# A hand-written issue order for TensorE, VectorE and ScalarE in the first layer of a graph network

## The chip, the cores and the metric

One core of a Trainium2 chip. The time is the device time of one execution in microseconds; the kernel before took 6855.91 us, the median of three runs (6827.99 to 6860.81). In the profile PE is TensorE (PEld its weight loads), DVE VectorE, ACT ScalarE, POOL GpSimd (here: it issues gathers), SP SyncE (here: it issues the other transfers).

## The reference, cut to what matters

Two layers of a graph network over 3125 nodes of 256 features and 100000 edges. The change is in layer 0, whose first half adds two independent parts to `x`:

```python
def transformer_conv(x, edge_index, ...):          # twice, each followed by batch norm and leaky ReLU
    q, k, v = (x @ wq + bq), (x @ wk + bk), (x @ wv + bv)       # 4 heads of 64
    alpha = jnp.sum(q[dst] * k[src], axis=-1) / math.sqrt(out_ch)
    # softmax of alpha over the edges of each dst node
    out = jax.ops.segment_sum(v[src] * alpha[..., None], dst, num_segments=n)
    return out + x @ ws + bs

for i in range(4):                                  # the linear attention, "mix"
    h = _layernorm(x, ln1_g[i], ln1_b[i])
    # q: softmax over features, k: softmax over tokens; context = k^T v, out = q context
    x = x + _linear_attn(h, Wq[i], Wk[i], Wv[i], Wo[i], bo[i])
    h = _layernorm(x, ln2_g[i], ln2_b[i])
    x = x + (gelu(h @ W1[i] + b1[i]) @ W2[i] + b2[i])
```

After that come a routed mixture of experts and layer 1, which the change leaves alone.

## The kernel before, in words

Everything is float32. The kernel is written against a framework with a scheduler: the program states instructions and their tiles, and the scheduler decides the order in each engine's queue. At run time each engine goes through its queue in order and waits on semaphores.

**The convolution.** Nodes are sorted by degree and packed 128 to a tile, 25 tiles (`SLOTS` has the number of edge slots of each, 64 down to 22, 833 in all). `by_slots` goes over the tiles; `steps` cuts a tile's slots into 2 to 4 steps of one or two halves of up to `SUB` = 8 slots, 63 steps and 115 halves for each convolution. For each slot `gather` (L635) issues one indirect transfer on POOL that brings the 128 rows `k|v` of the edges' sources into a buffer `kv` of 8 slots. There are four `kv` buffers. On a half, DVE multiplies the keys by the query (L926) and sums over features into `al` (L930). On a step, DVE adds the bias, takes the maximum and subtracts it (L939, L943, L944), ACT takes the exponential (L952), DVE sums it into `den` (L953). On a half again, DVE multiplies the values by the weights (L959) and adds pairs of slots (L965), and PE adds the slots up with an identity matmul into `acc` (L968), which frees the `kv` buffer. ACT copies `acc` into `res` (L972). At the tile's end the steps are joined (L978 to L999), and `done` adds the skip product on PE (L1101, L1107), ACT adds the bias, and SP stores `hsp`. Between the convolutions the batch norm, and for each tile a product with the next `k|v` weights that POOL scatters into `kvtab2`; after the second, a transpose and a scatter into `gout`.

**The linear attention** runs beside it. `l0_mix_groups` is a generator over 4 layers and 7 groups of up to 4 row tiles of 125, in two passes for each layer: norm and transposes (`norm_T`, L1176 to L1195), keys with exponential (L1234, L1241), queries and values (L140), the context (L1269), the softmax of the queries, stored to DRAM as `qd` through ACT's queue; then join, attention output (`add`, L1202), norm, the 1024-wide gelu (L1339, L1343) and the second product (L140, L1202). `by_slots` calls `beside` once a step, which lets the generator state a rated number of its units. This sets only where the units stand in the program: the scheduler then merges both into each engine's queue by its own priorities and estimates.

Both parts share PE, DVE and ACT. PSUM has four banks for the attention (`mm`), two for the convolution's sums (`cps`) and two for queries (`qa`).

Of the kernel before, what the change touches and what calls it, by code (L numbers as in the profile page):

```python
# [10 lines left out]
F32 = mybir.dt.float32  # L11
# [8 lines left out]
P = 125  # L20
# [805 lines left out]

class Beside:
# [46 lines left out]
def by_slots(k, order, kvtab, heads, scale, pl, wq, bq, inputs, done, edge=None, fill=None, beside=None):  # L874

# [9 lines left out]
    wide = 2 * SUB * heads  # L885
# [3 lines left out]
    if edge is not None:  # L889
        qq = pq.tile([128, 2, D], F32, name="qa", tag="qa")  # L890

    def prepare(i):
        qa = pq.tile([128, 512], F32, name="qa", tag="qa") if edge is None else None
        q = qq[:, i % 2] if qa is None else qa[:, :D]
        xpT = inputs(i, None if qa is None else qa[:, D:])
        for ci in range(2):
            nc.tensor.matmul(q, xpT[:, ci], wq[:, ci], start=(ci == 0), stop=False)
        nc.tensor.matmul(q, k.ones_row, bq, start=False, stop=True)
        return qa, q, xpT

    for i, ns in enumerate(SLOTS):
        st = steps(ns)
        nC = len(st)
        for t in range(3 * (i == 0) or 1) if fill is not None else ():
            if i + 2 * (i > 0) + t < len(SLOTS):
                fill(i + 2 * (i > 0) + t)
        qa, q, xpT = prepare(0) if i == 0 else ahead
# [4 lines left out]
        for c, subs in enumerate(st):  # L912
# [4 lines left out]
            if edge is not None:  # L917
                add_edges = edge(i, s0, S)
            for m in subs:
# [4 lines left out]
                if edge is not None:  # L924
                    add_edges(kv, b0, m)
# [21 lines left out]
            if edge is None:  # L947
                lo = D + c * wide % D
                w3 = qa[:, lo : lo + S * heads].rearrange("p (s h) -> p s h", h=heads)
            else:  # L950
                w3 = a2
# [22 lines left out]
            if beside is not None:  # L974
                beside()
# [15 lines left out]
        if edge is None:  # L991
            share = qa[:, : nC * heads].rearrange("p (c h) -> p c h", h=heads)
        else:
            share = mx[:, :nC]
# [11 lines left out]
def l0_weights(k, pool, a, n):  # L1006


    nc = k.nc
    wkv = pool.tile([128, 2, 2 * D], F32, name="wkv", tag="wkv")  # L1010
    bkv = pool.tile([128, 2 * D], F32, name="bkv", tag="bkv")
    for j, nm in enumerate("kv"):
        nc.sync.dma_start(
            wkv[:, :, j * D : j * D + D], a[f"w{n}{nm}"].rearrange("(c p) m -> p c m", p=128)
        )
        nc.sync.dma_start(bkv[:, j * D : j * D + D], a[f"b{n}{nm}"].partition_broadcast(128))
    one = lambda f, nm, tag: f(k, pool, a[nm], tag)
    return (
        wkv, bkv, load_w(k, pool, a[f"w{n}q"], f"wq{n}"), load_row(k, pool, a[f"b{n}q"], f"bq{n}"),
        load_w(k, pool, a[f"w{n}s"], f"ws{n}"), load_col(k, pool, a[f"b{n}s"], f"bs{n}"),  # L1020
        load_col(k, pool, a[f"g{n}"], f"gam{n}"), load_col(k, pool, a[f"be{n}"], f"bet{n}"),
    )
# [12 lines left out]
def l0_gnn_slots(k, dram, order, a, y, pp, pq, cw, beside, tmp):  # L1035
# [11 lines left out]
    ws = {1: l0_weights(k, cw, a, 1)}  # L1047
    with ExitStack() as st:
# [11 lines left out]
        wkv, bkv = ws[1][:2]  # L1060
# [12 lines left out]
    ws[2] = l0_weights(k, cw, a, 2)  # L1073
    kvtab2 = dram.tile([NQ * 128, 2 * D], F32, name="kvtab2")
    bst = cw.tile([128, 2, NQ, 6], F32, name="bst")
# [3 lines left out]
    for n in (1, 2):  # L1079
        wq, bq, wsk, bs, gam, bet = ws[n][2:]  # L1080
        hsp = dram.tile([128, NQ, 2, 128], F32, name=f"hsp{n}")
        with ExitStack() as st:
            gp, wp = pl(st, ("c_kv", 4), ("c_wk", 2))

            def inputs(i, ps):
                if n == 1:
                    return rows_T(k, wp, ps, ytab, order.near[:, i : i + 1])
                h = wp.tile([128, 2, 128], F32, name="xg", tag="xg")
                nc.sync.dma_start(h, prev[:, i])
                t = wp.tile([128, 2, 128], F32, name="xpT", tag="xpT")  # L1090
                norm_cols(k, t, h, sc, sh)
                return t

            def done(i, res, nC, xpT):
                ps = pp.tile([128, 512], F32, name="cps", tag="cps")
                o = wp.tile([128, 2, 128], F32, name="o1", tag="o1")
                mm = None
                for c in range(2):
                    ch = slice(c * 128, c * 128 + 128)
                    for s in range(nC):  # L1100
                        m1 = nc.tensor.matmul(  # L1101
                            ps[:, ch], res[:, s, ch], k.ident, start=(s == 0), stop=False
                        )
                        if s == 0 and mm is not None:
                            after(k, m1, [mm])
                    for ci in range(2):
                        mm = nc.tensor.matmul(  # L1107
                            ps[:, ch], wsk[:, ci, ch], xpT[:, ci], start=False, stop=(ci == 1)
                        )
                for c in range(2):  # L1110
                    nc.scalar.activation(
                        o[:, c], ps[:, c * 128 : c * 128 + 128], AF.Identity,
                        bias=bs[:, c : c + 1], scale=1.0,
                    )
                    nc.vector.bn_stats(bst[:, c, i], o[:, c, : min(128, N - i * 128)])
                nc.sync.dma_start(hsp[:, i], o)

            by_slots(
                k, order, (kvtab1, kvtab2)[n - 1], 4, 0.125, (gp, wp, pp, "cps", pq), wq, bq,
                inputs, done, fill=order.fill if n == 1 else None, beside=beside,  # L1120
            )
        prev = hsp
        for c in range(2):
            nc.vector.bn_aggr(bmv[:, c], bst[:, c])
        nc.scalar.activation(sc, bmv[:, :, 1], AF.Sqrt, bias=k.eps, scale=1.0)
        nc.vector.reciprocal(sc, sc)
        nc.vector.tensor_tensor(sc, sc, gam, op=ALU.mult)
        nc.vector.tensor_tensor(sh, bmv[:, :, 0], sc, op=ALU.mult)
        nc.vector.tensor_tensor(sh, bet, sh, op=ALU.subtract)
        with ExitStack() as st:  # L1130
            big, wp = pl(st, ("c_h", 1), ("c_rows", 4))
            h = big.tile([128, NQ, 2, 128], F32, name="h")
            for g0 in range(0, NQ, 5):
                nc.sync.dma_start(h[:, g0 : g0 + 5], hsp[:, g0 : g0 + 5])
            if n == 2:
                gout = dram.tile([NQ * 128, D], F32, name="gout")
            wkv, bkv = ws[2][:2]
            sent = []
            for i in range(NQ):
                norm_cols(k, h[:, i], h[:, i], sc, sh)  # L1140
                ps = pp.tile([128, 512], F32, name="cps", tag="cps")
                if n == 1:
                    t = wp.tile([128, 2 * D], F32, name="kvrow", tag="kvrow")
                    for c in range(2):
                        nc.tensor.matmul(ps, h[:, i, c], wkv[:, c], start=(c == 0), stop=(c == 1))
                    nc.vector.tensor_tensor(t, ps, bkv, op=ALU.add)
                    put_rows(k, kvtab2, order, i, t, sent)
                else:
                    t = wp.tile([128, D], F32, name="row", tag="row")
                    for c in range(2):  # L1150
                        nc.tensor.transpose(ps[:, c * 128 : c * 128 + 128], h[:, i, c], k.ident)
                    nc.scalar.copy(t, ps[:, :D])
                    put_rows(k, gout, order, i, t, sent)
# [6 lines left out]
def l0_mix_groups(k, dram, a, y, wts, one, wp, hp, pp):  # L1160
# [3 lines left out]
    nc, N, NT = k.nc, k.N, k.NT  # L1164
    scale = 32.0 ** -0.25
    NG = len(k.groups)
    ps_tile = lambda: pp.tile([128, 512], F32, name="mm", tag="mm")

    def norm_T(g0, ng, g, b):

        st = wp.tile([P, 4, 6], F32, name="ln_st", tag="ln_st")
        mv = wp.tile([P, 4, 2], F32, name="ln_mv", tag="ln_mv")
        rs = wp.tile([P, 4], F32, name="ln_rs", tag="ln_rs")
        nm = wp.tile([P, 4], F32, name="ln_nm", tag="ln_nm")
        for j in range(ng):
            nc.vector.bn_stats(st[:, j], y[:, g0 + j])  # L1176
            nc.vector.bn_aggr(mv[:, j], st[:, j])
        nc.scalar.activation(rs[:, :ng], mv[:, :ng, 1], AF.Sqrt, bias=k.eps[:P], scale=1.0)
# [22 lines left out]
    def add(i, ps):  # L1201
        nc.vector.tensor_tensor(y[:, i], ps, y[:, i], op=ALU.add)  # L1202

    for l in range(4):
# [118 lines left out]
        for gi, (g0, ng) in enumerate(k.groups):  # L1323
# [12 lines left out]
            for j in range(8):  # L1336
# [9 lines left out]
                if j % 2:  # L1346
                    yield
# [1366 lines left out]
```

## Time and profile before

| what | value |
|---|---|
| median of three runs | 6855.91 us |
| the profiled execution | 6843.34 us, its span 6841.6 us |
| granted TensorE clock, mean | 0.812 of full speed |
| busy over the span | PE 4761 us (70%), DVE 4259 (62%), POOL 2895 (42%), ACT 1565 (23%) |
| first gather of the first convolution | 303 us |
| between the convolutions | 1815 to 1880 us |
| last scatter of layer 0's convolutions | 3462 us |

The page shows the span in slices and the costliest groups of instructions; busy time of PE is counted from pipelined matmuls and is not PE at its peak. Every float32 product of the program shows as two records. The idle time of an engine before an instruction is put down to what released that instruction.

### The profile page before, as it was taken

How to read it: one execution, taken by the hardware profiler on the slowest of the kernel's cores; microseconds unless marked ns; L12 is line 12 of the kernel's file. 1: busy time of each engine (PE TensorE's matmuls, PEld its weight loads, DVE VectorE, ACT ScalarE, POOL GpSimd, SP SyncE). 2: the span in 40 equal slices, each digit the busy share in tenths (PEclk: the TensorE clock that was granted, in tenths of full speed). 3: DMA queues.
4: the chain of work that ended last, by engine and by line, in shares of the span. 5: the costliest groups of instructions: out<-in, count | busy, mean ns of one | idle time of the engine just before them, and what ended most of it. 6: DMA issues, size and time to landing. Idle time of an engine off the chain costs nothing. (4 is left out here: it accounts for less than half of the span.)

```text
span 6841.6 us, 48524 instructions
## 1 busy us (share of the span) xinstructions
PE 4761.2 (70%) x15819; PEld 2715.8 (40%) x15819; DVE 4259.0 (62%) x6249; ACT 1565.2 (23%) x3160; POOL 2894.6 (42%) x2947
## 2 busy tenths in 40 slices
PE   3444887578855797668837757777887877787639
PEld 2233654345533464445525523333333333333215
DVE  5277767666666777767632256666776566667571
ACT  2111223223312233223321102222222222121111
POOL 2456655555455555555442134334443333333210
PEclk9767988789978898779858878788888878777769
DMA  4356555545455555555444354333443333343310
GB/s 137 93 151 188 174 146 167 165 145 156 148 162 158 161 170 158 166 152 161 143 147 130 113 163 127 93 108 116 131 129 119 112 115 104 113 129 111 99 34 20
DMA packets 374153, 908.38 MB, mean 133 GB/s; under 512 B 94264, under 2 KB 169946, under 8 KB 373764
## 3 DMA queue, kind: packets, MB, share of 16 engines
q0 software_dynamic: 232624, 725.48, 36.7%
q1 hardware_dynamic: 132740, 155.30, 7.1%
q10 hardware_dynamic: 8526, 24.39, 0.9%
q8 instruction: 128, 2.10, 0.1%
q14 instruction: 135, 1.11, 0.1%
HBM read 813.50 MB, written 91.30 MB: 132 GB/s over the span
## 5 line engine op out<-in xcount | busy, mean ns | idle before, releaser
L635 POOL DMA_INDIRECT kv<-kvtab,slots x2499 | 2438.8, 976 | 2411.5 <-PE acc L968 819.8
L926 DVE TENSOR_TENSOR kv<-kv,qa 128x1792 f32<-128x1792 f32 (+2 forms) x345 | 716.6, 2079 | 359.8 <-DMA kv<-kvtab,slots 298.4
L2042 DVE TENSOR_TENSOR kv<-kv,e 128x1024 f32<-128x1024 f32 (+1 forms) x448 | 505.4, 1140 | 469.2 <-PE e L2037 199.6
L930 DVE TENSOR_REDUCE al<-kv 128x28 f32<-128x1792 f32 (+5 forms) x345 | 713.1, 2075 | 5.4 <-issue 3.8
L2037 PE MATMUL e<-weT,eaT 128*128 128x512 f32 (+1 forms) x896 | 552.4, 714 | 196.7 <-ACT eaT L2036 98.9
L968 PE MATMUL cps<-kv,ident 128*128 128x256 f32 x1792 | 506.7, 437 | 162.5 <-DVE kv L965 73.6
L968 PEld LDWEIGHTS cps<-kv,ident 128*128 128x128 f32 x1792 | 381.9, 221 | 269.5 <-issue 101.9
L959 DVE TENSOR_TENSOR kv<-kv,qa 128x1792 f32<-128x1792 f32 (+2 forms) x230 | 472.1, 2076 | 0.0
L1339 PE MATMUL mm<-hTm,w 128*128 128x500 f32 (+1 forms) x896 | 389.2, 593 | 64.2 <-issue 34.2
L140 PE MATMUL mm<-w,hid 128*125 128x256 f32 x1600 | 377.6, 387 | 11.8 <-issue 10.9
L965 DVE TENSOR_TENSOR kv<-kv 128x768 f32<-128x768 f32 (+1 forms) x345 | 350.8, 1044 | 1.1 <-DVE cw L1320 1.1
L2037 PEld LDWEIGHTS e<-weT,eaT 128*128 128x128 f32 (+1 forms) x896 | 161.6, 218 | 438.4 <-issue 227.1
L140 PEld LDWEIGHTS mm<-w,hid 128*125 128x125 f32 x1600 | 299.4, 190 | 83.2 <-issue 37.7
L968 PE MATMUL acc<-kv,ident 128*128 128x256 f32 x896 | 257.4, 449 | 67.4 <-DVE kv L965 62.4
L1339 PEld LDWEIGHTS mm<-hTm,w 128*128 128x128 f32 x896 | 175.5, 211 | 260.8 <-issue 211.1
L968 PEld LDWEIGHTS acc<-kv,ident 128*128 128x128 f32 x896 | 200.2, 229 | 146.7 <-DVE kv L965 89.4
L2036 ACT COPY eaT<-e 128x128 f32<-128x128 f32 (+1 forms) x448 | 110.1, 266 | 583.0 <-PE e L2034 265.9
L959 DVE TENSOR_TENSOR kv<-kv,al 128x1792 f32<-128x1792 f32 (+2 forms) x115 | 235.1, 2082 | 0.0
L140 PE MATMUL mm<-wqv,hTm 128*125 128x512 f32 x400 | 224.8, 669 | 5.2 <-DVE qs L1259 5.2
L2034 PE MATMUL e<-ident,ea 128*128 128x128 f32 (+1 forms) x448 | 131.8, 326 | 98.7 <-DVE kv L2042 50.9
L2475 PE MATMUL w<-x,sel 32*128 32x500 f32 (+3 forms) x448 | 168.1, 694 | 45.9 <-ACT sq L2480 28.1
L1234 PE MATMUL mm<-hTm,wk 128*128 128x500 f32 (+1 forms) x224 | 121.3, 684 | 104.7 <-ACT hTm L1195 69.5
(394 smaller groups left out, 7486.1 us busy)
## 6 DMA issues: line engine op xcount, KB each, us to landing
kv<-kvtab,slots POOLq DMA_INDIRECT x2499
w<-in_L_ffn_w_dram SPq DMA_DIRECT2D x32, 512.0 KB
qd<-qT ACTq DMA_DIRECT2D x24, 500.0 KB
kvtab<-st SPq DMA_DIRECT2D x12, 1000.0 KB
qT<-qd SPq DMA_DIRECT2D x24, 500.0 KB
xTg<-xcols SPq DMA_DIRECT2D x24, 500.0 KB
w<-in_L_mix_W_dram SPq DMA_DIRECT2D x8, 1024.0 KB
xs<-zero SPq DMA_DIRECT2D x16, 512.0 KB
```

Source lines behind the costliest of these rows:

```text
L140: nc.tensor.matmul(ps, lhs(c), w(c), start=(c == 0), stop=(bias is None and c == n_chunks - 1))
L635: return k.nc.gpsimd.indirect_dma_start(out=out, out_offset=None, in_=table, in_offset=bass.IndirectOffsetOnAxis(ap=index, axis=0),)
L926: nc.vector.tensor_tensor(kv[:, :m, :D], kv[:, :m, :D], q.unsqueeze(1).to_broadcast([128, m, D]), op=ALU.mult,)
L930: nc.vector.tensor_reduce(al[:, b0 : b0 + m], hv(kv[:, :m, :D]), axis=AX.X, op=ALU.add)
L959: nc.vector.tensor_tensor(v, v, w3[:, b0 : b0 + m].unsqueeze(3).to_broadcast([128, m, heads, d]), op=ALU.mult,)
L965: nc.vector.tensor_tensor(v, v, kv[:, half : 2 * half, D:], op=ALU.add)
L968: nc.tensor.matmul(acc[:, :D], k.ident, kv[:, j, D:], start=(b0 + j == 0), stop=(kv is bufs[-1][2] and j == left[-1]),)
L1339: nc.tensor.matmul(ps[:, :w_], w1[:, c, j * 128 : j * 128 + 128], hT[:, c, :w_], start=(c == 0), stop=(c == 1),)
L2034: nc.tensor.transpose(e[r, 0, :128], ea[:, c0 : c0 + n * 64], k.ident)
L2037: nc.tensor.matmul(e[:, :n].rearrange("p b d -> p (b d)"), eaT[r], weT[r, :n].rearrange("p b d -> p (b d)"), start=True, stop=True,)
L2042: nc.vector.tensor_tensor(t, t, e[:, :n].unsqueeze(2).to_broadcast([128, n, 2, D]), op=ALU.add)
L2475: nc.tensor.matmul(ps[:f, b, :w_], sel[rows, t * 128 : t * 128 + f], qT[rows, :w_], start=True, stop=True, tile_position=((h0 + b) * 32, 0),)
```

## The change

The three engines PE, DVE and ACT get, in the layer-0 stretch, the order in which the program states instructions (`k.tc.manual_schedule(engines=ORDERED)`); POOL and SP stay with the scheduler. For that the program is restated.

- `SlotOrder` replaces `by_slots` for layer 0 and states the steps as a software pipeline: the gathers of step n+1 ahead of step n, the first half's keys of step n+1 at the end of step n, a tile's join and output in the first step of the next tile. Layer 1 keeps `by_slots`.
- `l0_mix_pieces` cuts the attention into pieces: a PE part (`pe`), a closing part on DVE or ACT (`post`), a weight in us of PE time and the pieces that must be closed before.
- `Filling` puts pieces at three places in each step (twice 63 steps) and at one in each of the 25 tiles between the convolutions, by a rate that uses them up at the end. It looks at most 8 pieces ahead for one that may start, and states a piece's closing part behind the next piece's PE part.
- Smaller edits: the context's diagonal blocks alone are kept (32 columns instead of 128), two row tiles of attention output are added at once, `qd` is stored by SP instead of ACT, keys and values have four buffers instead of two, `hTm` two instead of one, and the second convolution's query and skip weights load into the first's buffers.

```diff
+class Filling:
+    def __init__(self, pieces, points, window=8):
+        self.todo, self.window, self.last = list(pieces), window, None
+        self.rate, self.due = sum(p.w for p in self.todo) / points, 0.0
...
+    def one(self):
+        for at, p in enumerate(self.todo[: self.window]):
+            if all(d.done for d in p.deps):
+                break
+        else:
+            return None
+        self.todo.pop(at)
+        if p.pe is not None:
+            p.pe()
+        self.flush()
+        self.last = p
+        return p
+
+    def __call__(self, share=1.0):
+        self.due = min(self.due + share * self.rate, 3.0 * self.rate)
+        while self.due > 0.0:
+            p = self.one()
+            if p is None:
+                self.flush()
+                break
+            self.due -= p.w
...
+class SlotOrder:
...
+        for n, t in enumerate(self.steps):
...
+            if n + 1 < len(self.steps):
+                self.gathers(n + 1)
+            if two:
+                self.keys(n, 1)
+            self.softmax(n)
+            if t["last"]:
+                self.join_max(i)
+            mix()
+            if c == 1:
+                self.q[i + 1] = make()
+            self.values(n, 0)
+            if before:
+                self.join(i - 1)
+            mix()
+            if before:
+                before["out"][0]()
+            if two:
+                self.values(n, 1)
+            if t["last"]:
+                self.join_sum(i)
+            if n + 1 < len(self.steps):
+                self.keys(n + 1, 0)
+            self.result(n)
+            if c == 0:
+                turn()
+            mix()
+            if before:
+                before["out"][1]()
+            if c == 0:
+                bring()
...
-def l0_mix_groups(k, dram, a, y, wts, one, wp, hp, pp):
+def l0_mix_pieces(k, dram, a, y, wts, one, wp, hp, hp2, pp):
+    us = lambda cols: cols * 1.7e-3
+    small = 0.3
...
+            K = [Piece(us(2 * w_), fn(keys, c), fn(keys_exp, c), [*ts, start, *before["X"]]) for c in range(2)]
+            Q = [Piece(us(1024), fn(qv, j), fn(qv_out, j), [*ts, *before["R"], *before["C"]]) for j in range(ng)]
...
+            Wp = [Piece(us(2 * w_), fn(inner, j), fn(inner_out, j), [*h["ts"], *freeh]) for j in range(8)]
+            O = []
+            for j in range(ng):
+                O.append(Piece(us(1024), fn(outer, j, 0), None, Wp))
+                O.append(Piece(us(1280), fn(outer, j, 1), fn(outer_out, j), Wp))
...
-        units = l0_mix_groups(k, dram, sub("L0_mix_"), y, wts, one, mwp, hp, pp)
-        beside = Beside(units, 8 * NT + 28 * len(k.groups), 2 * sum(len(steps(n)) for n in SLOTS))
-        gout, sent = l0_gnn_slots(k, dram, order, sub("L0_gnn_"), y, cp, pq, cw, beside, tmp)
-        beside.rest()
+        pieces = l0_mix_pieces(k, dram, sub("L0_mix_"), y, wts, one, mwp, hp, hp2, pp)
+        gout, sent = l0_gnn_slots(
+            k, dram, order, sub("L0_gnn_"), y, cp, pq, cw, lambda n: Filling(pieces, n), tmp
+        )
...
+    mix = filling(2 * 3 * sum(len(steps(n)) for n in SLOTS) + NQ)
+    with k.tc.manual_schedule(engines=ORDERED):
+        mix.ahead(30.0)
```

## The prediction

> **What bounds the kernel now.** First the page's busy shares and slices: no engine is full over the span, and the first half of it (layer 0) looks the same throughout. The stretch that the change touches is layer 0's graph convolutions with the linear attention beside them, from the first gather (302 us) to the last scatter (3470 us); so second the windows of that stretch. The columns are length, busy time of PE, weight loads, DVE, ACT and POOL, granted clock, DMA share and GB/s.
>
> ```profile
> 302.00:1815.00 1513.00, 1028.05 (x3728) 692.10 (x3728) 1037.64 (x1441) 377.24 (x721) 839.90 (x858) 0.82 0.55 159
> 1815.00:1880.00 65.00, 62.62 (x203) 34.90 (x203) 41.14 (x110) 36.20 (x86) 24.35 (x25) 0.97 0.54 194
> 1880.00:3410.00 1530.00, 1086.86 (x3896) 725.54 (x3896) 1076.46 (x1542) 429.23 (x826) 822.30 (x836) 0.83 0.54 158
> 3410.00:3470.00 60.00, 23.99 (x105) 14.00 (x104) 13.74 (x34) 33.40 (x88) 25.64 (x26) 0.60 0.72 269
> ```
>
> Each convolution has 63 slot steps, so the 3043 us of the two long windows are 24.2 us a step. In it DVE is busy 16.8, PE 16.8 at a granted clock of 0.82, and POOL must issue 13.2 gathers at 0.95 plus 0.30 us of issue, 16.5. Three engines each need some 17 of 24 us: nothing is full, they wait for each other. Third, the waits of the two windows (first pair: first convolution, second: second).
>
> ```profile
> POOL kv L635 <- PE cps L968: 282.9, 34, 25.3
> DVE kv L926 <- DMA kv<-kvtab,slots: 149.2, 36, 7.5
> POOL kv L635 <- PE cps L968: 358.8, 40, 24.9
> DVE kv L926 <- DMA kv<-kvtab,slots: 149.2, 36, 10.0
> ```
>
> This is a ring. A gather needs a free `kv` buffer (four), which the accumulating matmuls L968 free; PE runs them late; POOL stands for up to 25 us; then DVE waits for the rows. The timeline of one such place shows why PE is late:
>
> ```profile
> 2315.58 0.18 DVE L995 TENSOR_TENSOR qa<-mx,top 128x12 f32<-128x12 f32 x1
> 2316.27 3.62 PE L140 MATMUL mm<-w,hid 128*125 128x256 f32 x16
> 2320.44 3.72 PE L140 MATMUL mm<-w,hid 128*125 128x256 f32 x16
> 2324.71 3.72 PE L140 MATMUL mm<-w,hid 128*125 128x256 f32 x16
> 2325.00 2.29 DVE L926 TENSOR_TENSOR kv<-kv,qa 128x2048 f32<-128x2048 f32 x1 [9.24 <-PE mm L142]
> ```
>
> 12 us of the attention's matmuls stand in one lump while DVE has nothing for 9.24 us. Lumps on one engine, idling on the next.
>
> **The change, part by part.** DVE's work in the four windows is 1037.6+41.1+1076.5+13.7 = 2169 us. In the changed program's instruction order less of the attention stands ahead of the first gather (12 instead of 25 row statistics, 8 instead of 16 query tiles, and so on); at the rows' durations (0.41+0.17, 0.84 and 2.5 us a group) some 27 us more fall into the stretch. Removed: 56 context updates of 128 columns at 0.34 become 32 wide, like the 0.2 us rows of 128x28 to 128x64 (8 us); 100 attention adds of 256 columns at 0.418 become 52 of 512 at 0.69, the row of L1146 (6 us). So 2182. About 70 of them lie between the convolutions (25 adds of 0.69 and a share of the attention) and 14 at the end: 2098 us, 16.6 a step.
>
> The slot step is now a fixed chain on DVE: second key product and sum (4.15), the small softmax operations (0.65), first value product and pair sum (3.1), the same for the second half, the next step's first key product and sum, with three places for attention pieces. On PE every place holds about 3.3 us (1345 us of pieces by the code's own weights of 1.7 ns a column, over 403 places; the trace has 13.68 us for 32 records of 500 columns, 1.7 ns a column too). The value matmuls therefore wait behind at most one place of pieces, not behind 12 us. A buffer of the second half is free some 16 us after the step's start; its refill waits for POOL to end the first half's (by 20), takes 7.2x1.25 = 9 us plus landing and is there near 32; it is read two steps on, at 38 to 40. That leaves 6 us or more. Most of the 298 us that DVE waits for gathers should go; I keep 50. POOL then has 1666 + 50 gathers x 1.25 = 2145 us of issue and cannot be passed.
>
> What is late next is DVE's own waits, since it may not reorder any more.
> - Softmax: DVE computes `al`, ACT the exponential, DVE the sum L953. Without a table load this took 0.3 us (2330.85 to 2331.13), with one 1.6 (load 1.28, exponential 0.2, two hops). The changed order has a load before 75 of the 126; 55 of them have under 0.4 us of DVE work between. Counted through: 70 us bare, and half a gelu (0.68) of ACT occupied each time, 40. Bounds 50 and 220 (all bare). I take 110. Behind the waiting sum stand both value products and thereby PE and POOL.
> - ACT loads rise from 184 to 214 in layer 0, 38 us on an engine that is busy 26%; covered except for the above.
> - The 53 reciprocals after a square root and 27 query norms: mostly other DVE work between, 30 us (0 to 100).
> - Attention pieces that end on DVE (308 of some 1000). At the first place PE has run ahead. At the middle place PE first does the value matmuls (8 x 0.226) and then the piece (1.7), so DVE waits up to 3 us; at the third some 1. With 0.4 such a step: 126x0.4x4 = 200 us. The trace has no such wait in this order; bounds 60 (PE ahead) and 126x0.8x4 = 400; I take the middle, as both rows of PE are near.
> - Filling and draining the two convolutions: 50.
>
> Steps: 2098+110+30+200+50+50 = 2538 us, 20.1 each. Between the convolutions each of 25 tiles now holds a place: (1.7+3.3)x25 = 125 plus 15 for the batch norm, 140 instead of 65; the end stays 60. Sum 2738 against 3168: 430 us less. SP gets the 28 query stores from ACT's queue (0.3 us issues; SP is nearly idle): nothing, at most 28x2 us if they hold a weight load. The second convolution's query and skip weights now load between the convolutions into the same buffers, behind the last use: 0, at most 10. Layer 1 has the same instruction order on every engine, so the 3372 us after 3470 stay. The profiled run took 6843.3, its span 6841.6; 6843-430 = 6413. The median of the runs is 12.6 higher, so I say 6420.
>
> A rule against this: the clock. In the trace, stretches with PE busy 48 to 58% were granted 0.70 to 0.78, those with 87 to 92% 0.93 to 0.96; at 14 of 20 us I expect some 0.85, which PE's idle third covers. The Trainium skill, "TensorE: Matmul & The Clock Gate", Part 1, says that a gap of about 3.4 us takes the clock to half; by it a gap in every step would make PE's 13.8 us of full clock up to 28, and nothing would be won. A second rule, on the table loads: the trace has load and exponential back to back (2310.36+1.28, 2311.66). The Trainium skill, "ScalarE: Activation LUTs", What ACT_TABLE_LOAD costs, adds a drain of 1.38 us to the 1.28; 75 of them would be an estimated 100 us more.
>
> **The rivals.**
> 1. *Nearly all waits hide* (0.14). ACT and PE run ahead, only 160 us of waits stay: 2098+160+50+200 = 2508, 660 us less, 6180. For it: ACT is 26% busy. Against: 55 softmaxes have nothing between. POOL's 2145 gives the floor, 6070.
> 2. *PE becomes the ring* (0.14). The clock stays at 0.75 because PE gaps once a step: 16.8x0.82/0.75 = 18.3 plus a gap of 4 (PE has run out of pieces while DVE is at the first value product and pair sum) is 22.3 us: 2810+50+200 = 3060, 108 us less, 6735. The 0.70 of the first window speaks for it, that PE idles only where it is ahead against it.
> 3. *Slower: the fixed order joins all three queues* (0.10). An exponential stands on ACT behind gelus that wait for matmuls, which stand on PE behind value matmuls that wait for that exponential's DVE successors. If each place costs DVE 2.7 us: 16.6+8.1+0.9 = 25.6, x126+250 = 3476, 308 us more, 7150. It decides from 23.2 us a step ((3168-250)/126), 1.9 us at each place. Against it: a piece's closing operation stands behind the next piece's matmuls, and two thirds of them don't end on DVE.
> That the order is not taken as written is excluded by the instruction order.
>
> **How the numbers follow.** My forecast, the DVE-bound step of 20 us, has 0.62, by itself 6260 to 6600 (the bounds of the waits). With the first rival below and the second above, 8 in 10 lie between 6180 and 6740. A measurement tells about 0.5% (34 us) from no change: faster 0.88 (forecast, rival 1 and most of 2), same 0.02, slower 0.10.
>
> **What would show it.** Right: waits of POOL for the accumulating matmuls under 200 us in all (now 642), of DVE for gathers under 100 (now 298), DVE busy over 80% of the two long windows, which sum to some 2540 us, waits of the `den` sum near 110 and of the attention's adds near 200, a gap of 140 us between the convolutions. Wrong: gathers still waited for, a granted clock below 0.78, or DVE standing for PE over 2 us at each place.

## The result and the profile after: slower by 3.3%

The changed kernel took 7061.47 us (median of four, 7055.84 to 7099.71) against 6848.78 for the kernel before beside it: 1.0326, 95% interval 1.028 to 1.0371. The profiled execution has a span of 7054.4 us (before 6841.6). Predicted were 6420 us and a range of 6180 to 6740. Times of different chips differ by up to a tenth here (the kernel before took 6170 us on one of them), so every ratio below is against the kernel before on the same chip.

First the windows of the stretch, cut at the same events and with the same columns as before the change (length, busy PE, weight loads, DVE, ACT, POOL, granted clock, DMA share, GB/s):

```profile
284.00:1905.00 1621.00, 1074.44 (x3839) 732.93 (x3840) 1130.45 (x1544) 420.13 (x829) 831.72 (x858) 0.80 0.51 151
1905.00:2045.00 140.00, 124.19 (x440) 69.06 (x438) 70.11 (x172) 79.54 (x177) 25.29 (x26) 0.95 0.26 90
2045.00:3625.00 1580.00, 1041.50 (x3693) 716.32 (x3694) 1100.05 (x1450) 405.97 (x797) 807.22 (x836) 0.80 0.54 159
3625.00:3685.00 60.00, 23.58 (x74) 12.73 (x72) 14.17 (x36) 30.43 (x80) 25.12 (x25) 0.53 0.46 163
```

The steps became longer, 25.7 and 25.1 us, 3201 us in all where it was 3043. In them DVE is busy 2230 us (2114 before) and idle 971 (929 before). So the idle time that the order was expected to halve is all still there, and 116 us of work came on top. With the gap between the convolutions (140 instead of 65) and an earlier first gather (285 instead of 303) that is 116+42+75-18 = 215 of the 213 us between the spans. What follows layer 0's convolutions takes 3369 us (3372 before).

What DVE waits for is different, though. Three views of the changed kernel's waits over the stretch, of DVE, PE and POOL (who waits, for what; us in total, times, longest):

```profile
DVE xcur L1846 <- PE mm L1843: 128.5, 29, 13.0
DVE xcur L1846 <- remote: 88.1, 13, 11.9
DVE qm L1612 <- ACT vs L1610: 84.9, 35, 8.3
DVE xcur L1797 <- PE mm L1789: 84.4, 21, 6.4
DVE kmx L1590 <- PE mm L1580: 53.6, 17, 6.2
DVE kv L1103 <- DMA kv<-kvtab,slots: 46.2, 12, 20.0
```
```profile
PE cps L1146 <- DVE kv L1143: 605.6, 110, 15.0
```
```profile
POOL kv L635 <- PE cps L1146: 711.8, 85, 22.6
```

The wait for gathered rows is nearly gone (46 us, it was 298). In its place DVE stands before the closing operations of the attention's pieces (L1846, L1797, L1612 and L1590: in the two long windows 605 us together), and PE stands 605.6 us before the value matmuls, for DVE's pair sum. That the two sums are equal is chance (in e_first PE's falls and DVE's grows): of DVE's 605 us some 300 were ended by PE by this profile and some 90 by ACT; for the rest the profile names no instruction. POOL waits more than before for the buffers that those matmuls free (642 us before). Some steps of it in the timeline, POOL and weight loads left out:

```profile
2408.51 1.89 PE L1789 MATMUL mm<-cw,qT 128*125 128x256 f32 x8
2411.67 0.23 DVE L1116 TENSOR_TENSOR al<-al,bias 128x64 f32<-128x64 f32 x1
...
2415.20 1.23 DVE L1143 TENSOR_TENSOR kv<-kv 128x1024 f32<-128x1024 f32 x1
...
2416.48 3.78 PE L1146 MATMUL cps<-kv,ident 128*128 128x256 f32 x8 [6.08 <-DVE kv L1143]
...
2425.69 2.29 DVE L1106 TENSOR_REDUCE al<-kv 128x32 f32<-128x2048 f32 x1
...
2430.53 2.06 ACT L1500 ACTIVATE xh<-xcur,ln_nm,ln_rs 125x256 f32<-125x256 f32 x4
```

PE has done its piece at 2410.4 and then stands for 6.08 us: next in its queue are the value matmuls, and DVE is still at the keys, the softmax and the value product. The attention's matmuls stand behind them in the queue and may not pass. Later it is the other way round: DVE has ended the keys at 2428, and the row below shows it idle for 5.19 us before a batch norm statistic whose input stands on ACT behind two gelus and four `xh`; the keys of the step's second half stand behind it and start at 2434.81:

```profile
2433.44 0.55 DVE L1403 BATCH_NORM_STATS2 bst<-o 128x6 f32<-128x128 f32 x2 [5.19 <-ACT o L1398]
```

### The profile page after: what moved, and what is told of

The parts are those of the page before. It is cut to its first block, busy times and chain, and to the rows that moved or that the text cites. A ratio compares the mean times of both kernels' runs of the same rounds, so it can differ in the third digit from the quotient of the medians.

```text
span 7054.4 us, 48601 instructions
## 1 busy us (share of the span) xinstructions
PE 4825.3 (68%) x15819; PEld 2773.5 (39%) x15819; DVE 4380.2 (62%) x6201; ACT 1599.0 (23%) x3276; POOL 2866.7 (41%) x2947
## 5 line engine op out<-in xcount | busy, mean ns | idle before, releaser
L1146 PE MATMUL cps<-kv,ident 128*128 128x256 f32 x1792 | 632.2, 513 | 760.1 <-DVE kv L1143 605.6
L1146 PEld LDWEIGHTS cps<-kv,ident 128*128 128x128 f32 x1792 | 440.3, 257 | 923.4 <-DVE kv L1143 662.6
L1106 DVE TENSOR_REDUCE al<-kv 128x28 f32<-128x1792 f32 (+2 forms) x230 | 479.4, 2084 | 7.9
L1838 PE MATMUL mm<-w,hid 128*125 128x256 f32 x1600 | 401.8, 403 | 14.3 <-issue 14.2
L1838 PEld LDWEIGHTS mm<-w,hid 128*125 128x125 f32 x1600 | 317.4, 203 | 79.8 <-issue 29.7
L2559 PEld LDWEIGHTS e<-weT,eaT 128*128 128x128 f32 (+1 forms) x896 | 164.5, 222 | 452.5 <-issue 247.0
L1143 DVE TENSOR_TENSOR kv<-kv 128x768 f32<-128x768 f32 (+1 forms) x230 | 241.8, 1051 | 8.0
L1153 ACT COPY res<-cps 128x256 f32<-128x256 f32 x126 | 46.7, 371 | 873.7 <-PE cps L1146 561.4
L984 DVE TENSOR_REDUCE al<-kv 128x56 f32<-128x1792 f32 (+2 forms) x115 | 238.7, 2076 | 1.8 <-issue 0.9
L140 PE MATMUL mm<-wqv,hTm 128*125 128x512 f32 x400 | 200.3, 646 | 17.1 <-ACT kT L1592 9.1
```

Of the source, the lines that this page charges most:

```text
L140: nc.tensor.matmul(ps, lhs(c), w(c), start=(c == 0), stop=(bias is None and c == n_chunks - 1))
L1106: nc.vector.tensor_reduce(t["al"][:, b0 : b0 + m], self.heads(kv[:, :m, :D]), axis=AX.X, op=ALU.add)
L1143: nc.vector.tensor_tensor(v, v, kv[:, half : 2 * half, D:], op=ALU.add)
L1146: nc.tensor.matmul(t["acc"][:, :D], self.k.ident, kv[:, j, D:], start=(b0 + j == 0), stop=(b == len(t["subs"]) - 1 and j == left[-1]),)
L1838: nc.tensor.matmul(ps[:P, :D], s["hid"][:, c, j * P : j * P + P], W["w2"][:, c, :], start=(c == 0), stop=False,)
L2559: nc.tensor.matmul(e[:, :n].rearrange("p b d -> p (b d)"), eaT[r], weT[r, :n].rearrange("p b d -> p (b d)"), start=True, stop=True,)
```

## The experiments

Three theories for a start. *Place*: the middle place is the costly one (the prediction's own reason). *Clock*: PE's gaps lower its granted clock, and its matmuls are slow for that. *Order*: the queues, each fixed, hand work to each other in turn.

**e_first: all pieces at the first place.** `mix(3.25)` there, none at the others, and the cap of a place raised from 3 to 6 shares.

> All attention pieces of a step at the first place, behind the softmax (3.25 shares there, none at the second and third; the cap on owed work raised from 3 to 6 shares). Theory 1, order: DVE stands for TensorE because at the second and third place a piece's matmuls come after the value matmuls that DVE has only just released, so DVE reaches the closing operation first. At the first place TensorE has some 9 us of lead: the waits of the closing operations (626 us) and of the batch norm statistics (151 us) fall under 250 us in all, time 6550 to 6750. Theory 2, clock: TensorE is late because it stands idle for 6 us in each step and then runs at half clock; ten us of pieces behind the second value matmuls fill the gap as well, so the time falls likewise, and the value matmuls' mean falls from 513 to under 450 ns. If neither holds, the lump delays the value matmuls as it did before the change, gathers are waited for again and the time stays at 7000 or more.

Measured: 1.0368 (1.0272 to 1.0464). DVE idles 755 us before the closings, against 651 counted alike in the changed kernel (all attention tiles). So moving all pieces to the place with the most lead doesn't help. PE's wait for the pair sum did fall, from 606 to 364 us, and the closings waited longer all the same: part of their wait is the attention's own chain, here through ScalarE (`xh`). What the first place then looks like:

```profile
2420.91 1.94 PE L1508 MATMUL mm<-ident,xh 125*128 125x125 f32 x4 [5.17 <-ACT xh L1498]
...
2432.22 0.42 DVE L1844 TENSOR_TENSOR xcur<-mm,xcur 125x256 f32<-125x256 f32 x1 [14.98 <-remote]
```

DVE waits 15 us for one addition while all value products of the step stand behind it.

**e_warm: ten idle products ahead of a step's value matmuls**, to keep PE's clock up.

```diff
+            for _ in range(10):
+                nc.tensor.matmul(
+                    t["acc"][:, D:], self.k.ident, self.wide, start=True, stop=True
+                )
```

> The changed kernel with ten idle products of 128x256 ahead of each step's first value matmuls, into the unused half of the sum's PSUM bank (4.3 us at full clock, work that leaves the output as it is). Theory 2, clock: the value matmuls' mean falls from 513 to some 440 ns, the pieces behind them run at full speed, the waits of the closing operations fall from 626 to under 400 us, time 6750 to 6900. Theory 1, order: the granted clock rises but the waits stay, time 7000 to 7100. If the idle products overrun the gap, they add up to 1 us a step, 7150.

Measured: 1.0329 (1.0268 to 1.0389), the same. The windows show that the edit did what it was to do:

```profile
285.00:1905.00 1620.00, 1306.92 (x5085) 941.52 (x5086) 1128.94 (x1540) 420.11 (x829) 830.76 (x857) 0.88 0.51 150
2045.00:3605.00 1560.00, 1260.26 (x4990) 912.01 (x4988) 1104.74 (x1462) 409.41 (x806) 812.31 (x837) 0.90 0.55 163
```

The clock went from 0.80 to 0.88 and 0.90 and the value matmuls' mean from 513 to 436 ns, as the clock theory asked, but the steps stayed, and so did DVE's idle time before the closings (627 us, 626 in the changed kernel, both with those between the convolutions). A gain of some tens of us could be hidden by the idle products themselves (PE is busy 451 us more and stands 376 us less before the value matmuls); the loss of 213 us isn't the clock's.

**e_lag2: a piece closes behind the matmuls of two following pieces** instead of one (places of 1.06 shares, cap 4). `flush(2)` closes all open pieces but the last two.

```diff
...
-        self.flush()
-        self.last = p
+        self.open.append(p)
+        self.flush(2)
...
```

> The changed kernel with a piece's closing operation behind the matmuls of the two next pieces instead of one (cap 4 shares, 1.06 shares a place so that the pieces still end with the steps). Theory 1, order: the closing operations then fall a place later, the waits fall from 626 to some 300 us, time 6700 to 6850. Theory 2, clock: TensorE is as late as before, waits fall by less than 150 us, time 6900 to 7050.

Measured: 1.0147 (1.0111 to 1.0183). Slack at the hand-over gives back about half of the loss; DVE idles 515 us before closings (651, counted alike, in the changed kernel), and PE's wait for the pair sum falls to 452.5. DVE's waits fell by 136 us, less than the order theory had said; it is e_warm that rules out the clock theory.

**e_sched: the restated program, all three engines left to the scheduler.**

```diff
-    with k.tc.manual_schedule(engines=ORDERED):
+    with ExitStack():
```

> The restated program (slot steps, pieces and places as changed) without the hand-written order: the scheduler orders all engines. If the loss comes from the fixed order, the time is near the kernel before, 6750 to 6900; if it comes from the restating (finer pieces, 30 more table loads, rate of the pieces), it stays near 7060.

Measured: 0.9904 (0.9872 to 0.9937), faster than both kernels.

```profile
298.00:1745.00 1447.00, 1000.10 (x3647) 686.50 (x3648) 1023.80 (x1431) 380.59 (x743) 834.16 (x857) 0.81 0.57 167
1863.00:3315.00 1452.00, 1009.81 (x3702) 691.07 (x3702) 1030.03 (x1437) 402.35 (x787) 813.23 (x837) 0.82 0.59 172
```

The steps take 23.0 us. The restated program is better; the fixed order costs more than it brings. DVE is busy 2054 us here and 2230 in the hand order, for nearly the same instructions (2868 records in these windows, 2994 there); more on this under e_nodve.

**e_noact, e_nope, e_nodve: one engine given back to the scheduler**, the two others as written (`ORDERED` without Activation, PE, DVE).

> ScalarE alone gets its scheduler back; TensorE and VectorE keep the hand order. All three free took 0.9904 of the kernel before, the hand order 1.0326: 290 us apart. Theory A (a ring through three queues: softmax on VectorE, exponential and the attention's closings behind it on ScalarE, the attention's matmuls on TensorE, its additions on VectorE): freeing any one of them lets the ring slip, so this gives back over half, under 6930 us, and ScalarE's wait for the subtraction L1120 (225 us) falls under 100. Theory B (VectorE's order is the cost: 130 us of lost overlap and 620 us of additions standing ahead of value products): under 60 us, over 7000. Theory C (ScalarE's order alone, exponentials with attention behind them): nearly all, under 6830.

> TensorE alone gets its scheduler back. Theory A: over half of the 290 us, under 6930, since TensorE could then go past a piece that waits for ScalarE. Theory B: under 60 us, over 7000. Theory C: under 60 us too, over 7000, since what it could run early hangs on ScalarE's queue. If TensorE's order were the whole cost (value matmuls behind pieces): under 6830, and the 605 us that its value matmuls wait for VectorE stay while VectorE's waits for it vanish.

> VectorE alone gets its scheduler back. Theory A: over half of the 290 us, under 6930. Theory B: nearly all of it, under 6830, VectorE busy 2060 us in the two long windows instead of 2230 (its operations overlap again), and no addition ahead of a value product that is ready. Theory C: under 60 us from the order of waits plus at most the overlap of 130.

Measured, on one chip: e_noact 1.0274 (1.023 to 1.0317), e_nope 0.9998 (0.9974 to 1.0021), e_nodve 1.0009 (0.9993 to 1.0026). Theory A, a ring that needs all three queues, falls with the first: ScalarE free is worth nothing that the intervals show. B and C, one engine's order alone, fall as well: PE free or DVE free each brings the time back to the kernel before's, some 70% of the way to the same program with all three free (0.985 to 0.990). But they do it in different ways. The stretches from the first to the last copy into `res` of each convolution, summed (e_noact, e_nope, e_nodve; the changed kernel itself was not run on this chip, so e_noact stands for the written order; length and busy times as above, the means are of the two stretches):

```profile
sum 2725.00, PE 2015.26 PEld 1389.42 DVE 2173.17 ACT 828.80 POOL 1578.75; mean PE 1007.63 PEld 694.71 DVE 1086.58 ACT 414.40 POOL 789.38
sum 2573.00, PE 1982.26 PEld 1356.13 DVE 2181.34 ACT 808.37 POOL 1586.48; mean PE 991.13 PEld 678.06 DVE 1090.67 ACT 404.19 POOL 793.24
sum 2568.00, PE 1959.26 PEld 1355.53 DVE 2040.74 ACT 809.56 POOL 1587.27; mean PE 979.63 PEld 677.77 DVE 1020.37 ACT 404.78 POOL 793.64
```

With PE free DVE has the same work (2173 and 2181 us) and is idle 392 us instead of 552: it waits less. With DVE free its idle time is nearly the same (527), and what is gained is 132 us of busy time (with 72 of 2954 instructions fewer in these stretches). So freeing PE opens the ring; freeing DVE is worth as much, but hardly by waiting less. The waits in the two convolutions show how. First e_noact, where the ring is intact, then e_nope, then e_nodve:

```profile
DVE xcur L1846 <- PE mm L1843: 150.8, 39, 7.5
DVE xcur L1797 <- PE mm L1789: 104.0, 31, 6.4
PE cps L1146 <- DVE kv L1143: 596.1, 145, 29.0
```
```profile
DVE xcur L1846 <- PE mm L1843: 56.0, 22, 7.8
PE cps L1146 <- DVE kv L1143: 92.8, 45, 7.4
```
```profile
DVE kv L1103 <- DMA kv<-kvtab,slots: 197.5, 56, 19.7
DVE xcur L1846 <- PE mm L1843: 25.5, 23, 4.1
PE cps L1146 <- DVE kv L1143: 399.3, 98, 19.9
```

A free PE runs attention matmuls while the pair sum is missing: its wait falls from 596 to 93 us, and DVE, still in its written order, stands less before the closings (L1846: 56 us, it was 151). A free DVE passes the closings that aren't ready (25.5 us at L1846); PE still stands 399 us, and DVE now waits for rows instead, 198 us where it was some 50 in e_noact. The page's total of DVE's busy time shows this second price of the fixed order over the whole run (e_nope, then e_nodve):

```profile
PE 4570.3 (74%) x15819; PEld 2659.2 (43%) x15819; DVE 4369.0 (71%) x6201; ACT 1590.6 (26%) x3276; POOL 2887.7 (47%) x2947
```
```profile
PE 4550.7 (74%) x15819; PEld 2658.7 (43%) x15819; DVE 4244.2 (69%) x6201; ACT 1592.7 (26%) x3276; POOL 2895.7 (47%) x2947
```

The same 6201 instructions occupy DVE 125 us less when the scheduler orders them. They aren't much shorter (their lengths add up to 4645 and 4628 us); the records of neighbours overlap more, 287 us in all in the written order and 395 in the scheduler's. In e_nope a record that follows at once and shares no tile name with the one before starts 82 ns before that one's end (median), one that shares a name 34 ns after it. The written order has 2551 such unrelated neighbours, the scheduler's 3374: it more often puts other work between an operation and the one that needs its result.

**e_alone: no attention inside the steps**; it runs at the 25 places between the convolutions and behind the second.

> The three places inside the steps hold no attention; the 25 places between the convolutions do, and the rest of it runs behind the second convolution. The hand order of the slot step by itself: VectorE's own work is 15.3 us a step (965 us over 63 steps), gathers 16.5 us on POOL. Theories A, B, C (the pieces between are the cost): 17 to 18 us a step, the two long windows 1070 to 1150 each, VectorE idle under 2 us a step; then some 1400 us of attention by itself, the whole 7300 to 7600. If the slot chain itself were slow (softmax and exponential bare, buffers refilled late): 20 us a step or more, windows over 1260.

Measured: 1.1612 (1.1564 to 1.166), 7147 us. By the copies into `res` a step takes 17.7 and 17.3 us, as expected, with PE's clock at 0.65; DVE is idle 2.5 us of it, where under 2 were expected. The rest of the attention by itself takes some 1445 us (2713 to 4159). The hand-written slot step is sound alone. What costs is the pieces between. (The expected total was for slower chips; on this one the kernel before took 6170 us.)

**e_again, e_sched5, e_noadd, e_onetable: sizes, on one chip.** e_noadd states neither of the additions L1797 and L1846; e_onetable has `AF.Identity` in place of `AF.Gelu` at L1828.

> The changed kernel once more, unaltered, beside the three below: chips differ by up to a tenth in time, so its ratio on this chip is what the others are held against. 1.03 as before, with steps of 25 us or a little less.

> The restated program with all three engines left to the scheduler, again, on the chip of the changed kernel. If its gain over the kernel before is of the program and not of one chip: 0.985 to 0.995, faster than both.

> Left out: the attention's two kinds of addition on VectorE that wait straight for TensorE (L1797 and L1846, 152 operations, some 77 us of work, 390 us of idle time before them in the changed kernel). The order of everything else stays written by hand. If VectorE standing at these places for TensorE is one arc of a ring of the two: 300 us back or more of the 213 that the change lost plus the 77 of work, that is at or under 0.99, and TensorE's wait for VectorE before the value matmuls (605 us) falls by half. If the waits only move to the next operation that needs TensorE (L1590, L1612): under 120 us, over 1.015.

> The attention's 224 gelus compute an identity instead, which needs no table of its own: the loads before gelus and before the exponentials behind them go (some 2 x 75 in layer 0, 190 us of ScalarE). If the loads and ScalarE's order are in the ring: 100 us back or more, 1.015 or less. If the ring is of TensorE and VectorE, and ScalarE is only passed through: 20 to 60 us, 1.02 to 1.03.

Measured: the changed kernel again 1.0296 (1.0275 to 1.0316); the scheduler's version 0.9848 (0.9827 to 0.9869), so its gain isn't of one chip. From the first to the last copies into `res` the changed kernel takes 3010 us (DVE busy 2181) and the scheduler's version 2706 (2001): of 304 us, 180 are DVE's busy time (with 131 of 2952 instructions fewer in these stretches) and 124 its idle time. e_onetable 1.0238 (1.0209 to 1.0267): 114 fewer table loads (211 to 97), 146 us of ScalarE, are worth 0.6%, some 40 us. e_noadd 1.0031 (1.0005 to 1.0057): 0.0265 or 179 us back, between the two expectations; PE's wait for the pair sum falls from 535 to 385 us, not by half. Before the two additions DVE idled 350 us, and they are 77 us of work, 427 in all. Where the other 248 went is in the groups of DVE (busy us, mean ns of one, idle before them and what ended it), e_again first:

```profile
L1131 DVE TENSOR_REDUCE den<-qa 128x4 f32<-128x56 f32 (+7 forms) x126 | 26.1, 207 | 63.2 <-issue 37.6 <-ACT qa L1125 24.0 <-ACT res L1153 1.2
L1403 DVE BATCH_NORM_STATS2 bst<-o 128x6 f32<-128x128 f32 (+1 forms) x98 | 25.9, 289 | 128.0 <-ACT o L1398 51.1 <-issue 31.9 <-ACT hid L1828 25.3
```
```profile
L1403 DVE BATCH_NORM_STATS2 bst<-o 128x6 f32<-128x128 f32 (+1 forms) x100 | 27.1, 290 | 263.0 <-ACT o L1398 138.4 <-issue 71.5 <-ACT res L1153 25.7
L1131 DVE TENSOR_REDUCE den<-qa 128x4 f32<-128x56 f32 (+7 forms) x126 | 26.3, 209 | 133.3 <-ACT qa L1125 71.5 <-issue 59.5 <-ACT res L1153 1.7
```

135 us moved to the next operation that waits in the fixed order, the batch norm statistic, 70 to the `den` sum and 40 to the norms' reciprocal (L1494). With one arc cut, the next ones carry over half of its wait.

**e_outer, e_outlag2, e_schedlag2**: no middle place (1.6 or 1.7 shares at the first and the third, caps 4 and 5), alone and with the late closings; and the late closings with all three engines free.

> No attention at the middle place, 1.6 shares each at the first and the third. Theory P (the prediction's own reason: the middle place, where TensorE does the value matmuls first, is the costly one): over half of the loss comes back, 1.015 or less. Theory R (two fixed queues that hand work over to each other, wherever the pieces stand): larger lumps at two places cost what three small ones did, 1.02 to 1.035.

> No middle place (1.7 shares at the two others), and each piece's closing operation behind the matmuls of two following pieces instead of one. Two following pieces at all three places gave 1.0147. Theory P: below 1.00. Theory R: the slack counts and not the place, 1.005 to 1.02.

> All three engines left to the scheduler, with closings behind two following pieces in the program's order. Where the engines may reorder, slack in the program's order should hardly count: 0.98 to 0.99, as without it (0.9848 and 0.9904). If the scheduler keeps near the program's order and waits at closings are left (345 us of VectorE standing before them in the first such run): 0.97 or less.

Measured, on one chip: 1.0355 (1.0301 to 1.041), 1.0247 (1.0192 to 1.0302) and 0.9897 (0.9864 to 0.993). Without the middle place the loss is undiminished, as in e_first: moving the pieces away from it doesn't help. Both runs also make the lumps larger, so what a place costs at equal lumps isn't shown apart. Late closings seem to help again (the intervals touch), but less than with three places, more than 1.02 where I had said less; that few large lumps use the slack up is my reading, not shown. With free engines the slack is worth nothing.

## Why the prediction was wrong, by its own steps

**The step that failed** is the closings term: "Attention pieces that end on DVE", 200 us with bounds of 60 and 400. Measured 605 us in the two long windows, 1.6 at each of 378 places, and 147 more before the batch norm statistic, which had no term. By the place at which DVE met them, the closings are 78 at the first place with 122 us of idle time, 105 at the middle with 343, 87 at the third with 141. So the price of the middle place was right (3.3 us each, "up to 3"), that of the third too low (1.6, "some 1"). Two things were wrong:

- *The count.* "0.4 such a step" has no working in the prediction; measured are 0.83 a step at the middle and 0.69 at the third, and its own 308 pieces over 403 places are 0.76. At the predicted prices the measured count gives 402 us, 202 more than the term: half of the 405 us that are missing.
- *The first place*, put at nothing because "PE has run ahead": 122 us, 1.6 each. Being ahead doesn't help in a fixed order: PE reaches the value matmuls early and stands there for DVE's pair sum (605.6 us, 110 times for 230 halves), with the pieces that DVE will ask for next queued behind. I had counted DVE's standing for PE, place by place, and never PE's standing for DVE. e_nope shows what that is worth: with PE free to pass, DVE is idle 160 us less at equal work.

The prices make up the other 82. And "the trace has no such wait in this order" overlooked the kernel before's own: DVE was idle 299 us before the same three kinds of closing in its stretch (L1202 126.1, L1258 90.4, L1239 82.9) and 73 before the statistic, with the scheduler at work. The fixed order was put at 200 and nothing.

I also took the middle place for the costly one. It was, with three places in use; but with it empty (e_first, e_outer) the waits stood at the others.

**DVE's work**: 2098 predicted, 2230 measured. I had carried over the busy time of the kernel before, as if an instruction's share of it were its own. It depends on the order, by how much neighbours overlap: e_nodve shows 125 us of difference at equal instructions.

The sum then closes. Steps 3201 against 2538, 663 more: work +132, closings +405, statistics +147, softmax -45 (65, predicted 110, within its bounds), gathers +12 (62, predicted 50), norms 0 (30), the rest, for which filling and draining had 50, +12.

**Right**: the gather waits go; between the convolutions 140 us, the end 60, layer 1 3369 (3372 predicted), each as worked out. The slot step by itself is sound too (e_alone). The first step of the working was right, but the waits of the kernel before were exchanged for others of the same size: DVE's idle time went from 929 to 971 us.

**The signs named**: DVE busy 70% of the long windows (over 80% was the sign of right), POOL's waits for the accumulating matmuls 712 (under 200), the attention's adds 385 (near 200). None of the three signs of wrong showed: gathers are hardly waited for, the clock is above 0.78, and DVE stands 1.6 us a place rather than over 2 (3.3 at the middle one). Wrong by 640 us, the forecast failed at less than I had thought it would take.

**The rivals.** The third came nearest, 25.6 us a step against 25.7 and 25.1, 7150 against 7061, and its outline (fixed queues that join) is what the runs show. Its mechanism was not: it led over exponentials on ACT, and giving ACT back (e_noact) or taking the loads away (e_onetable) changes little or nothing. What the runs show needs the orders of PE and DVE only; that the number came so near is luck. What I held against it, that a closing stands behind the next piece's matmuls, is one piece of slack, 1.7 us, against PE waits of 5.5 us on average (605.6 over 110); two pieces (e_lag2) were worth about half of the loss. The second rival had the gap right (6.08 us in the timeline) and drew the wrong conclusion: raising PE's clock didn't shorten the step.

**The two rules.** The records agree with the Trainium skill, "TensorE: Matmul & The Clock Gate", Part 1: the eight value matmuls took 3.78 us after the gap of 6.08. Others in the same stretch without a gap took 1.89:

```profile
2426.36 1.89 PE L1146 MATMUL cps<-kv,ident 128*128 128x256 f32 x8
```

But e_warm shows that it didn't decide the result here. On "ScalarE: Activation LUTs", What ACT_TABLE_LOAD costs: the page's drain doesn't show in the trace, where a gelu follows its load at once; 114 of the 211 loads were worth some 40 us together:

```profile
2412.73 1.28 ACT L1828 ACT_TABLE_LOAD   x1
...
2414.02 1.24 ACT L1828 ACTIVATE hid<-mm,b 128x500 f32<-128x500 f32 x2
```

**Open**: how the 605 us divide between TensorE's waits and the attention's own chains through ScalarE (the first eats into the second), whether the shorter busy time is by itself what e_nodve gained (no run changes it alone), and whether some written order with more slack, beyond what four `mm` banks allow, would reach the scheduler's.

## What to carry to other kernels

Before fixing the order of two engines that feed each other, follow the hand-over in both directions: for every place where B waits for A, ask what A itself stands before at that time, and what B will want that is queued behind it. Average slack says little; what counts is whether the work behind a standing instruction may go past it, and one engine of the two left free to reorder was enough here to get back to the kernel before (1.03 became 1.00). Don't carry an engine's busy time over to another order: a chain in which each operation needs the one before it took DVE longer than the same operations mixed with others. Test a hand order against the same program with the scheduler on: that was the fastest version of all (0.985 to 0.990), so the restating was worth having and the fixed order was not.

## What the runs showed of the hardware

Three things I had not expected. The same 6201 DVE instructions took 4369.0 us of busy time in the written order and 4244.2 in the scheduler's, 125 us less, on one chip, because records of neighbours that share no tile overlap (82 ns in the median) and those that share one mostly don't. Raising the granted clock from 0.80 to 0.88 by idle products changed the time by nothing measurable, and the steps without attention ran at 17.5 us with a clock of 0.65. And chips differ: with the same instruction order in layer 1 the last part of the program took 3369 us in the first run of the changed kernel, and 3033 (from 3300 us to the end) on the chip of e_noact, while DVE was busy 1957 and 1952 us in it, at a granted clock of 0.79 and 0.84; why was not looked into.
